# The last half blocks of a graph-attention layer: which engine normalises them, in which order GpSimd works, and where the block in front is put

## The chip, the cores and the metric

The kernel runs on one core of a Trainium2 chip. The core has five engines with a queue of instructions each: TensorE (PE in the profile; its weight loads are PEld), VectorE (DVE), ScalarE (ACT), GpSimd (POOL) and SyncE (SP), which here only issues DMAs. Each of VectorE, ScalarE, GpSimd and SyncE works its queue strictly in the order in which the program wrote it; an instruction that waits holds up all that stand behind it. Engines wait for one another by semaphores. The metric is the time of the whole program in microseconds (us), lower is better.

## The reference

One layer of masked attention on x (8 frames, 2048 nodes, 256 channels), eight heads of 32 channels, with a feed-forward part, two normalisations inside and one behind:

```python
scores = where(adj > 0, q @ k.T / sqrt(32), -1e9)        # per frame and head
t = softmax(scores) @ v
x1 = layernorm(x + t) * g1 + be1
h = relu(x1 @ w1 + b1)
x2 = layernorm(x1 + h @ w2 + b2) * g2 + be2
out = layernorm(x + x2)                                   # no scale, no shift
```

All is float32. A layernorm is (value - mean) / sqrt(variance + eps) over the 256 channels of a row.

## The kernel before, in words

The main loop runs over 1024 items: 8 frames, 4 blocks of 512 query rows, 2 groups of four heads, 16 blocks of 128 keys. Step t of the loop issues the exponential of item t+1 (ScalarE, L283), the scores of item t+2 (TensorE) with the addition of the mask (VectorE, L279), the product with the values of item t (TensorE, L310) and the sums of exponentials (GpSimd, L339, or an accumulating DMA). The very last group of heads of the last block, called ENDING, is done in two halves of 256 rows: its items 1008 to 1015 are half 0, 1016 to 1023 half 1, each item now covering two key blocks (scores L264 and L268, values L298, sums L330 and L332).

All other work stands in a list `fill` of Python generators, sorted by a due step. At the start of each step t, `advance(t)` goes through the list once. A generator that yields a number sleeps for so many steps; one that yields BANK needs a free bank of PSUM and TensorE time, and only one may have it in a step. `credit` limits that TensorE work to about one unit of 512 columns a step, unless some generator that wants a bank is past its due step: then no limit holds. A generator in the middle of a group of matmuls yields MORE, or WAIT for a step that is not there yet; it then is the `holder`, and while there is a holder at the start of a step nobody else gets a bank in that step. After step 1023 the list is worked off by `advance(t, finish=True)` for t = 1025, 1026 and so on, where any number of generators may have banks in one pass, still in the order of due steps. The order in which the passes write instructions is the order of the queues; times follow from that.

Three generators matter at the end:

- `tail` for the block in front (the third block of the last frame, whole, 512 rows; `xb` is set for it and for no other): normalise (`norm`, per=2), feed-forward, normalise, GpSimd's multiplication by g2 (L445) and addition of `xb`, which holds x + be2 (L447), normalise, store (L453). In `norm` VectorE takes statistics (L348, L349), GpSimd makes 1/sqrt and the bias (L353 to L357), ScalarE applies them (L360). `per` says how many of the four row tiles are done before it yields.
- `closing(0)` and `closing(1)`, the two halves of the last block, with due steps 1024 and 1023. Each sums its denominators on TensorE in five terms (L494) and adds them to those of the other heads (L497); turns them and the attention output, divides and adds x (L508, L526, L529); takes statistics (`half_stats`: L460, L461 on VectorE, L463, L464 on GpSimd); normalises (`half_norm`: L469, then ScalarE L471); has GpSimd make the residual for later (L535, L536) while TensorE turns the rows and ScalarE applies g1 and be1 (L541); does the two products of the feed-forward (L548 and L557, listed by the profile under the helper's line L54, with L549 between); adds the residual (L559), normalises, multiplies by g2 and adds x + be2 (L564, L565), normalises and stores (L569).

Each `yield` in `closing` ends its part of the pass. In the kernel before, half 0 gets through its denominators by step 1023, half 1 makes all its five terms in pass 1025, and half 0 is one part ahead of half 1 from there; in a pass, half 1's part is written in front of half 0's next part, because its due step is the earlier one.

Of the kernel before, what the change touches and what calls it, by code (L numbers as in the profile page):

```python
# [61 lines left out]
def fast_path(ctx, tc, cst, x, adj, out, RS):  # L62
# [339 lines left out]
    def outcome(f, qc):  # L402
        yield ROOM
        state["tails"] += 1
        xin = x[f, qc * CH:(qc + 1) * CH, :].rearrange("(p j) c -> p j c", p=P)
        y = yp.tile([P, TPC, C], F32, name="y")
        begin = items.index((f, qc, 1, LAST)) + SUM + 2
        yield from divide(f, qc, y)
        if (f, qc) == (F - 1, NCK - 2):
            xb = state["xb"]  # L410
            for j in range(0, TPC, 2):
                yield BANK
                ps = bank()
                columns(ps, ident, xb[:, j:j + 2, :].rearrange("p j c -> p (j c)"), start=True, stop=True)
                nc.vector.tensor_tensor(y[:, j:j + 2, :], ps.rearrange("p (j c) -> p j c", c=C), y[:, j:j + 2, :], ALU.add)
            start(begin + 4, tail(f, qc, y, xin, 2, xb), begin + 18)
            return
        nc.gpsimd.dma_start(y, xin, accum_op=ALU.add)
        if (f, qc) == (F - 1, NCK - 3):
            start(begin + 10, tail(f, qc, y, xin, 2), begin + 18)  # L420
        else:
            start(begin + 10, tail(f, qc, y, xin), begin + 26)
# [12 lines left out]
    def tail(f, qc, y, xin, per=1, xb=None):  # L435
        yield from norm(y, per)
        yield from feed_forward(y)
        if xb is not None:
            nc.gpsimd.tensor_tensor(xb, xb, rows(cst["be2r"]), ALU.add)
        yield 1  # L440
        z = y
        yield from norm(z, per if per == 1 else TPC)
        while xb is None and per > 1 and state["now"] % MB not in CALM:
            yield 1
        nc.gpsimd.tensor_tensor(z, z, rows(cst["g2r"]), ALU.mult)  # L445
        yield 1
        nc.gpsimd.tensor_tensor(z, z, rows(cst["be2r"]) if xb is None else xb, ALU.add)  # L447
        yield 1
        if xb is None:
            nc.gpsimd.dma_start(z, xin, accum_op=ALU.add)  # L450
            yield 7 if per == 1 else 10
        yield from norm(z, per)
        nc.sync.dma_start(out[f, qc * CH:(qc + 1) * CH, :].rearrange("(p j) c -> p j c", p=P), z)  # L453
        state["tails"] -= 1

    def half_stats(t):
        mv = small.tile([P, 2, nc.vector.BN_AGGR_DIM], F32, name="mv")
        for j in range(2):
            st = small.tile([P, nc.vector.BN_STATS_DIM], F32, name="st")
            nc.vector.bn_stats(st, t[:, j, :])  # L460
            nc.vector.bn_aggr(mv[:, j, :], st)  # L461
        rs = small.tile([P, 2], F32, name="rs")
        nc.gpsimd.tensor_scalar(rs, mv[:, :, 1], EPS, 1.0, op0=ALU.add, op1=ALU.mult)  # L463
        nc.gpsimd.tensor_tensor(rs, rs, cst["mhalf"][:, 0:2], ALU.pow)  # L464
        return mv, rs

    def half_norm(t, mv, rs):
        nb = small.tile([P, 2], F32, name="nb")
        nc.vector.scalar_tensor_tensor(nb, mv[:, :, 0], -1.0, rs, op0=ALU.mult, op1=ALU.mult)  # L469
        for j in range(2):  # L470
            nc.scalar.activation(t[:, j, :], t[:, j, :], AF.Identity, bias=nb[:, j:j + 1], scale=rs[:, j:j + 1])  # L471

    def closing(h):
        f, qc, g = ENDING
        own, part, t0 = slice(2 * h, 2 * h + 2), slice(h * HQ, (h + 1) * HQ), len(items) - MB // 2 * (2 - h)
        terms = [(5, 6), (1, 7), (0, 7), (6, 8), (7, 8)]
        dst = out[f, qc * CH + h * HQ:qc * CH + (h + 1) * HQ, :].rearrange("(p j) c -> p j c", p=P)

        def row2(v):
            return v[:, None, :].to_broadcast([P, 2, C])  # L480

        yield BANK
        ps = bank()
        for n, (block, when) in enumerate(terms):
            if n:
                yield MORE
            while state["now"] < t0 + when:
                yield WAIT
            term = PT.pop((*ENDING, block + h * MB // 2))
            state["credit"] -= 4 * CH  # L490
            for b in range(2):
                for i in range(4):
                    r = D * i
                    nc.tensor.matmul(ps[r:r + D, 0:HQ], cst["halves"][:, g, :], term[:, i, b * HQ:(b + 1) * HQ],  # L494
                                     start=(n + b == 0), stop=(n + b == len(terms)))
        dT = DT[f, qc]
        nc.vector.tensor_tensor(dT[:, part], ps[:, 0:HQ], dT[:, part], ALU.add)  # L497
        if h == 0:
            state["y"] = yp.tile([P, TPC, C], F32, name="y")
            state["ff"] = [work.tile([P, 2, CH], F32, name=n) for n in ("turned", "hT")]  # L500
        y, (yT, hT) = state["y"][:, own], state["ff"]
        xr, xb = (t[:, own] for t in state["rows"])
        def turned_sums():
            ps = bank()
            transposes(ps, [dT[:, part][:, j::2] for j in range(2)])
            den = ps[:, 0:HQ].rearrange("p (j c) -> p j c", c=P)[:, :, ::D // 2]
            rc = op.tile([P, 2, H], F32, name="rc")
            nc.vector.reciprocal(rc, den)  # L508
            return rc, den

        def count(den):
            nc.vector.tensor_tensor(RS[:, 0, own], RS[:, 0, own], den, ALU.add)
            nc.vector.tensor_tensor(RS[:, 1, own], RS[:, 1, own], den, ALU.min)

        yield 1
        if h == 0:
            yield BANK
            rc, den = turned_sums()
            count(den)
        yield BANK  # L520
        po = bank()
        transposes(po, [OT[f, qc, gg][:, part][:, j::2] for gg in range(2) for j in range(2)])
        if h:
            rc, den = turned_sums()
        for gg in range(2):
            nc.vector.tensor_tensor(y[:, :, gg * P:(gg + 1) * P].rearrange("p j (h d) -> p j h d", d=D),  # L526
                                    po[:, gg * HQ:(gg + 1) * HQ].rearrange("p (j h d) -> p j h d", h=4, d=D),
                                    rc[:, :, gg::2, None].to_broadcast([P, 2, 4, D]), ALU.mult)
        nc.vector.tensor_tensor(y, y, xr, ALU.add)  # L529
        found = half_stats(y)  # L530
        if h:
            count(den)
        yield 1
        half_norm(y, *found)
        nc.gpsimd.tensor_tensor(xr, y, row2(cst["g1r"]), ALU.mult)  # L535
        nc.gpsimd.tensor_tensor(xr, xr, row2(cst["be1b2r"]), ALU.add)  # L536
        yield BANK
        ps = bank()
        transposes(ps, [y[:, j, a * P:(a + 1) * P] for a in range(2) for j in range(2)])
        for a in range(2):  # L540
            nc.scalar.activation(yT[:, a, part], ps[:, a * HQ:(a + 1) * HQ], AF.Identity,  # L541
                                 bias=cst["be1c"][:, a:a + 1], scale=cst["g1c"][:, a:a + 1])
        yield 1
        for d in range(2):
            yield BANK
            ps = bank()
            for a in range(2):
                columns(ps[:, 0:HQ], w1s[:, a, d * P:(d + 1) * P], yT[:, a, part], start=(a == 0), stop=(a == 1))  # L548
            nc.scalar.activation(hT[:, d, part], ps[:, 0:HQ], AF.Relu, bias=cst["b1s"][:, d:d + 1], scale=1.0)  # L549
        yield 1  # L550
        yield BANK
        ps = bank()
        for j in range(2):
            if j:
                yield MORE
            for d in range(2):
                columns(ps[:, j * C:(j + 1) * C], hT[:, d, part][:, j * P:(j + 1) * P], w2s[:, d, :], start=(d == 0), stop=(d == 1))  # L557
        z = y
        nc.vector.tensor_tensor(z, ps.rearrange("p (b c) -> p b c", c=C), xr, ALU.add)  # L559
        found = half_stats(z)  # L560
        yield 1
        half_norm(z, *found)
        yield 1
        nc.vector.tensor_tensor(z, z, row2(cst["g2r"]), ALU.mult)  # L564
        nc.vector.tensor_tensor(z, z, xb, ALU.add)  # L565
        found = half_stats(z)
        yield 1
        half_norm(z, *found)
        nc.sync.dma_start(dst, z)  # L569

# [39 lines left out]
    def start(t, gen, due):  # L610
        fill.append([t, gen, 1, due])
        fill.sort(key=lambda e: e[3])
# [408 lines left out]
```

## Time and profile before

| | us |
|---|---|
| median of 3 runs | 3159.01 (3158.67 to 3160.27) |
| profiled execution, its own time | 3158.02 |
| its span, first to last instruction | 3156.0 |
| TensorE busy in the span | 3051.3 (97%), granted clock 0.994 |
| last exponential (L283) starts | 3110.35 |
| last matmul of the feed-forward (L54) ends | 3140.05 |
| last store (L569) is issued | 3151.15 |

Times inside the execution are counted from the start of the span. A row of the timeline gives start, duration, engine, line, operation, output<-input with their shapes, the number of instructions merged, and in brackets how long the engine had been idle before and what released it. What lies behind about 3110 us is the end of the program: no exponentials are left, and only the three generators above run.

### The profile page before, as it was taken

To read this page: it belongs to the slowest core of one execution; us is meant where nothing else is said; L and a number is where in the kernel's file an instruction comes from. 1 tells how busy PE (TensorE), PEld (TensorE's weight loads), DVE (VectorE), ACT (ScalarE), POOL (GpSimd) and SP (SyncE) were. 2 spreads that over 40 slices of the span, in tenths; PEclk is the share of its full clock that TensorE was granted. 3 is DMA by queue.
4 is the path that set the end of the run, shared out by engine and by line. 5 is a ranking of instruction groups with operands and counts; after the bars stand their busy time and mean duration, and the time that the engine had idled before them with its cause. 6 is when DMAs were issued, how large, how long until landed. Compare 5 with 4: busy or idle time off the path is not lost.

```text
span 3156.0 us, 68508 instructions
## 1 busy us (share of the span) xinstructions
PE 3051.3 (97%) x28988; PEld 962.6 (31%) x28988; DVE 2747.6 (87%) x3139; ACT 2427.1 (77%) x1934; POOL 2727.7 (86%) x1389
## 2 busy tenths in 40 slices
PE   8999999999999999999999999999999999999986
PEld 4222333233332233223332323323333233322223
DVE  4989888998888988888988888988888988889885
ACT  4877878777778877778777878778778778778774
POOL 1768989888889888899888899899989899899985
PEclk9999999999999999999999999999999999999998
DMA  8998878889789888789878899788888889778871
GB/s 258 223 210 185 196 170 194 193 191 198 173 174 209 197 190 178 170 195 214 192 169 187 187 207 195 166 184 204 197 176 191 190 192 202 167 173 166 173 157 42
DMA packets 165465, 586.86 MB, mean 186 GB/s; under 512 B 15360, under 2 KB 84480, under 8 KB 116512
## 3 DMA queue, kind: packets, MB, share of 16 engines
q0 software_dynamic: 63696, 430.60, 69.4%
q1 hardware_dynamic: 100640, 150.50, 14.1%
q8 instruction: 229, 3.75, 0.5%
q10 hardware_dynamic: 816, 1.31, 0.1%
q14 instruction: 84, 0.69, 0.1%
HBM read 146.15 MB, written 37.75 MB: 58 GB/s over the span
## 4 chain that ended last, share of the span: by engine, by line


## 5 line engine op out<-in xcount | busy, mean ns | idle before, releaser
L279 DVE TENSOR_TENSOR p<-s,mask 128x1024 f32<-128x1024 f32 x2016 | 2371.5, 1218 | 297.7 <-PE s L276 123.4
L283 ACT ACTIVATE p<-p 128x2048 f32<-128x2048 f32 x1024 | 1955.7, 1910 | 551.1 <-DVE p L279 449.1
L339 POOL TENSOR_TENSOR p<-p 128x2048 f32<-128x2048 f32 x409 | 1999.9, 4890 | 221.3 <-ACT p L283 200.4
L276 PE MATMUL s<-qT,kT 32*128 32x512 f32 x8064 | 1152.0, 640 | 56.5 <-DVE p L279 52.6
L310 PE MATMUL x<-p,v 128*32 128x512 f32 x8064 | 1075.8, 606 | 5.8 <-ACT p L283 4.2
L276 PEld LDWEIGHTS s<-qT,kT 32*128 32x128 f32 x8064 | 315.3, 183 | 659.5 <-DVE p L279 629.4
L336 POOL DMA_DIRECT2D p<-p x378 | 416.2, 1104 | 49.2 <-ACT p L283 41.0
L310 PEld LDWEIGHTS x<-p,v 128*32 128x32 f32 x8064 | 158.7, 108 | 771.3 <-issue 315.1
L54 PE MATMUL x<-in,wqkv 128*32 128x512 f32 x1888 | 245.7, 592 | 0.0
L383 PE MATMUL x<-p,halves 128*32 128x512 f32 x1768 | 231.1, 594 | 1.6 <-DVE kT L170 1.4
L360 ACT ACTIVATE y<-y,nb,rs 128x256 f32<-128x256 f32 x372 | 218.3, 591 | 0.5 <-POOL nb L357 0.5
L348 DVE BATCH_NORM_STATS2 st<-y 128x6 f32<-128x256 f32 x372 | 154.8, 416 | 0.0
L54 PE MATMUL x<-turned,w1s 128*32 128x512 f32 (+1 forms) x1008 | 125.2, 593 | 0.0
L54 PEld LDWEIGHTS x<-wqkv,in 128*32 128x32 f32 x3584 | 102.4, 110 | 66.5 <-issue 55.4
L54 PE MATMUL x<-w2s,hT 128*32 128x256 f32 x2048 | 122.0, 379 | 0.0
L54 PE MATMUL x<-wqkv,in 128*32 128x128 f32 x3584 | 118.2, 273 | 0.0
L54 PEld LDWEIGHTS x<-in,wqkv 128*32 128x32 f32 x1888 | 61.3, 110 | 141.3 <-issue 116.0
L354 POOL TENSOR_TENSOR rs<-rs,mhalf 128x4 f32<-128x4 f32 x93 | 96.2, 1035 | 7.8
L445 POOL TENSOR_TENSOR y<-y,g2r 128x1024 f32<-128x1024 f32 x31 | 99.3, 3205 | 2.2 <-ACT y L360 2.2
L383 PEld LDWEIGHTS x<-p,halves 128*32 128x32 f32 x1768 | 57.3, 110 | 133.9 <-issue 126.5
L447 POOL TENSOR_TENSOR y<-y,be2r 128x1024 f32<-128x1024 f32 x30 | 94.4, 3145 | 0.2
L54 PEld LDWEIGHTS x<-w2s,hT 128*32 128x32 f32 x2048 | 66.4, 110 | 69.7 <-issue 35.6
(164 smaller groups left out, 1433.6 us busy)
## 6 DMA issues: line engine op xcount, KB each, us to landing
p<-p POOLq DMA_DIRECT2D x380, 1024.0 KB, 9.1
in<-xd SPq DMA_DIRECT2D x87, 512.0 KB, 7.5
mask<-md SPq DMA_DIRECT2D x248, 128.0 KB, 5.4
y<-in_x_dram POOLq DMA_DIRECT2D x60, 512.0 KB, 10.3
out_dram<-y SPq DMA_DIRECT2D x31, 512.0 KB, 4.5
in<-in_x_dram SPq DMA_DIRECT2D x30, 512.0 KB, 6.8
xd<-in SPq DMA_DIRECT2D x28, 512.0 KB, 6.8
p<-in_adj_dram SPq DMA_DIRECT2D x8, 1024.0 KB, 14.3
```

Source lines behind the costliest of these rows:

```text
L54: nc.tensor.matmul(out[r:r + D], lhsT[:, r:r + D], rhs, start=start, stop=stop)
L276: nc.tensor.matmul(ps2[half][:, j, :], KT[f, mb // TPC, g][r:r + D, (mb % TPC) * P:(mb % TPC + 1) * P], QT[f, qc, g][r:r + D, :], start=Tr ...
L279: nc.vector.tensor_tensor(pt[:, 2 * half:2 * half + 2, :], ps, MK[f, qc, mb // 2][:, mb % 2, None, :].to_broadcast([P, 2, CH]), ALU.add)
L283: nc.scalar.activation(PT[item], PT[item], AF.Exp, scale=1.0 / math.sqrt(D))
L310: nc.tensor.matmul(O[grp][r:r + D, :], V[f, mb // TPC, g][:, mb % TPC, r:r + D], PT[item][:, h, :], start=(mb == 0), stop=(mb == LAST))
L336: nc.gpsimd.dma_start(PT[f, qc, g, chain[0]], PT.pop(item), accum_op=ALU.add)
L339: nc.gpsimd.tensor_tensor(first, first, PT.pop(item), ALU.add)
L348: nc.vector.bn_stats(st, t[:, j, :])
L354: nc.gpsimd.tensor_tensor(rs, rs, cst["mhalf"], ALU.pow)
L360: nc.scalar.activation(t[:, j, :], t[:, j, :], AF.Identity, bias=nb[:, j:j + 1], scale=rs[:, j:j + 1])
L383: nc.tensor.matmul(ps[r:r + D, :], cst["halves"][:, g, :], term[:, h, :], start=(n == 0), stop=(n == len(blocks) - 1))
L445: nc.gpsimd.tensor_tensor(z, z, rows(cst["g2r"]), ALU.mult)
```

## The change

Four things are edited, all of them at the end of the last frame.

1. The tail of the block in front is due at its begin + 14 (step 1011) instead of begin + 18 (step 1015).
2. In that tail, GpSimd's multiplication and addition are issued in the same step, and the last normalisation takes all four statistics in one step and applies all four in one (TPC is 4).
3. `half_norm` is two VectorE instructions (subtract the mean, multiply by 1/sqrt, with one number per row each) instead of one small VectorE instruction and two ScalarE activations. `closing` uses it three times per half; its middle use is dissolved: the mean and g2 are applied in one VectorE instruction per row tile without waiting for 1/sqrt, and 1/sqrt and x + be2 in a second one.
4. GpSimd's L535 and L536 are written behind the `yield 1` that follows the turning of the rows, so one pass later.

```diff
-            start(begin + 4, tail(f, qc, y, xin, 2, xb), begin + 18)
+            start(begin + 4, tail(f, qc, y, xin, 2, xb), begin + 14)
...
         nc.gpsimd.tensor_tensor(z, z, rows(cst["g2r"]), ALU.mult)
-        yield 1
+        if xb is None:
+            yield 1
         nc.gpsimd.tensor_tensor(z, z, rows(cst["be2r"]) if xb is None else xb, ALU.add)
         yield 1
         if xb is None:
             nc.gpsimd.dma_start(z, xin, accum_op=ALU.add)
             yield 7 if per == 1 else 10
-        yield from norm(z, per)
+        yield from norm(z, per if xb is None else TPC)
...
     def half_norm(t, mv, rs):
-        nb = small.tile([P, 2], F32, name="nb")
-        nc.vector.scalar_tensor_tensor(nb, mv[:, :, 0], -1.0, rs, op0=ALU.mult, op1=ALU.mult)
         for j in range(2):
-            nc.scalar.activation(t[:, j, :], t[:, j, :], AF.Identity, bias=nb[:, j:j + 1], scale=rs[:, j:j + 1])
+            nc.vector.tensor_scalar(t[:, j, :], t[:, j, :], mv[:, j, 0:1], rs[:, j:j + 1], op0=ALU.subtract, op1=ALU.mult)
...
         half_norm(y, *found)
-        nc.gpsimd.tensor_tensor(xr, y, row2(cst["g1r"]), ALU.mult)
-        nc.gpsimd.tensor_tensor(xr, xr, row2(cst["be1b2r"]), ALU.add)
         yield BANK
...
         yield 1
+        nc.gpsimd.tensor_tensor(xr, y, row2(cst["g1r"]), ALU.mult)
+        nc.gpsimd.tensor_tensor(xr, xr, row2(cst["be1b2r"]), ALU.add)
         for d in range(2):
...
-        found = half_stats(z)
-        yield 1
-        half_norm(z, *found)
-        yield 1
-        nc.vector.tensor_tensor(z, z, row2(cst["g2r"]), ALU.mult)
-        nc.vector.tensor_tensor(z, z, xb, ALU.add)
+        mv, rs = half_stats(z)
+        for j in range(2):
+            nc.vector.scalar_tensor_tensor(z[:, j, :], z[:, j, :], mv[:, j, 0:1], cst["g2r"], op0=ALU.subtract, op1=ALU.mult)
+        yield 1
+        for j in range(2):
+            nc.vector.scalar_tensor_tensor(z[:, j, :], z[:, j, :], rs[:, j:j + 1], xb[:, j, :], op0=ALU.mult, op1=ALU.add)
         found = half_stats(z)
         yield 1
         half_norm(z, *found)
```

## Prediction, made before the changed kernel was run

> **What bounds the kernel now.** The page's totals and slices come first.
>
> ```profile
> span 3156.0 us, 68508 instructions
> PE   8999999999999999999999999999999999999986
> ```
>
> TensorE is full in every slice but the ends; the change touches the last slice only, so I read that by the windows (busy time of PE, PEld, DVE, ACT, POOL, then the granted clock).
>
> ```profile
> 3110.00:3120.00 10.00, 7.67 (x120) 4.67 (x112) 2.51 (x8) 2.62 (x3) 4.73 (x2) 1.00 0.01 2
> 3120.00:3130.00 10.00, 2.21 (x7) 1.23 (x8) 6.30 (x29) 3.09 (x6) 4.65 (x7) 0.59 0.00 0
> 3130.00:3140.00 10.00, 10.00 (x133) 4.98 (x131) 1.44 (x4) 2.92 (x6) 3.81 (x6) 0.72 0.01 2
> 3140.00:3156.00 16.00, 0.24 (x8) 0.08 (x2) 7.42 (x25) 6.22 (x12) 4.36 (x8) 0.57 0.19 70
> ```
>
> Nothing is full but TensorE from 3130 to 3140, at 0.72 clock: the end is a chain across engines. The timeline, engine by engine, shows its links.
>
> ```profile
> 3113.18 4.50 PE L494 MATMUL s<-p,halves 128*32 128x256 f32 x80
> 3130.46 1.94 PE L54 MATMUL x<-turned,w1s 128*32 128x256 f32 x16
> ...
> 3117.75 0.43 DVE L497 TENSOR_TENSOR dT<-s,dT 128x256 f32<-128x256 f32 x1 [6.62 <-PE s L494]
> 3125.31 0.15 DVE L469 SCALAR_TENSOR_TENSOR nb<-mv,rs 128x2 f32<-128x2 f32 x1
> 3126.51 0.13 DVE L469 SCALAR_TENSOR_TENSOR nb<-mv,rs 128x2 f32<-128x2 f32 x1
> 3138.49 0.69 DVE L559 TENSOR_TENSOR y<-x,in 128x512 f32<-128x512 f32 x1 [11.85 <-PE x L54]
> ...
> 3128.50 1.08 ACT L471 ACTIVATE y<-y,nb,rs 128x256 f32<-128x256 f32 x2
> 3143.35 1.08 ACT L360 ACTIVATE y<-y,nb,rs 128x256 f32<-128x256 f32 x2
> ...
> 3121.69 0.71 POOL L464 TENSOR_TENSOR rs<-rs,mhalf 128x2 f32<-128x2 f32 x1
> 3129.66 1.27 POOL L535 TENSOR_TENSOR in<-y,g1r 128x512 f32<-128x512 f32 x1 [0.38 <-ACT y L471]
> 3146.19 0.54 POOL L463 TENSOR_SCALAR rs<-mv 128x2 f32<-128x2 f32 x1 [2.91 <-DVE mv L461]
> 3146.82 1.15 POOL L464 TENSOR_TENSOR rs<-rs,mhalf 128x2 f32<-128x2 f32 x1
> ...
> 3150.32 0.37 SPq L453 DMA_DIRECT2D out_dram<-y  x1
> 3151.15 0.33 SPq L569 DMA_DIRECT2D out_dram<-y  x1
> ```
>
> Half 0's 1/sqrt is ready at 3122.40 (3121.69+0.71), yet L469 starts at 3125.31: half 1's division, sum and statistics stand in front on VectorE. ScalarE then takes the norm of half 0, its turning, the norm of half 1, its turning; the feed-forward starts at 3130.46. Near the end the front block's L360 and its 512 KB store (L453) run among the halves' own.
>
> **The change, part by part.** I traced the generators by hand through `advance`.
>
> *The front block (due 1011, statistics at once).* At step 1013 it is past due, so the two last terms of the other heads' denominator go in one step and everything behind moves one step forward. Half 0's five terms come at 1018 to 1022 (1019 to 1023 before), three of half 1's go at 1023, and two are left for pass 1025. TensorE's work is the same. By its pitches (1.07 scores, 0.88 values, 0.97 a term) with the stall behind the front block's statistics (0.99, a step earlier), scores of item 1023 start at 3106.8 (3105.9 before). ScalarE's four L360 (2.06) now precede exponential 1022: values 1022 wait until 3110.2. Then values (0.88), three terms (0.87 each, from 4.50/5), values, two terms: the sums end at 3116.5, against 3117.68 before. **1.2 gained.** Queue by queue: GpSimd has L445 and L447 (2.36+2.37) behind the last L330 (about 3108.6), to 3113.5; VectorE's four statistics wait for that and end at 3115.6, in front of half 1's L497 (3116.5): 0.9 to spare. On SP the store moves from pass 1032 to 1028, ahead of both L569. The DMA L332, issued near 3102.3, lands within 8.4 (its longest), at 3110.7; its term wants it at 3112. GpSimd's L353 to L357 come before the halves' L463.
>
> *The halves' order.* Half 1 is the holder at the start of pass 1025, so half 0's turning waits for 1026. From there both run in the same pass, half 1 first. VectorE: L497 to L508 takes 1.0 (L497, two transposes); half 1's division, sum and statistics 2.86; its counts 0.14; half 0's, with counts, 0.48+1.52+1.09. Add 0.33 for the four small final-check instructions (L975 to L978) that also lie here now. That puts half 0's mean at 3124.0, its 1/sqrt 1.08 later, 3125.1.
>
> *Norms by VectorE.* No row has this form. L279 (1024 elements, two inputs) takes 1218 ns and L700 (a tensor_scalar, 1024) 691: the difference is half the streaming, so 164 fixed and 1.03 ns an element, half that in L700's fast form. For 256 elements: 296 ns if fast, 428 if not; with a per-row operand neither is shown. A pair at overlapped pitch is 0.5 or 0.76. I take the fast form, L700 being the same operation; the slow one costs 0.26 twice on the path. Half 1's norm hides behind half 0's 1/sqrt; ScalarE's two were 1.08. The scalar_tensor_tensor is taken at 0.42, L497's time for 256 elements (bounds 0.30 and 0.50).
>
> Here a rule speaks against the change. The row: L463 takes 0.54 at 3146.19 instead of 0.19, and L464 1.15 instead of 0.71, just where VectorE runs L564 and L565 with both inputs in SBUF; both end soon after a VectorE instruction does. The Trainium skill, page "SBUF — State Buffer", section "Who interferes with whom", says that GpSimd and a VectorE instruction with two SBUF inputs or in its two-port mode hold one port pair exclusively, whichever starts first. By the rows alone VectorE loses nothing; by the rule L535 (1.27), free to start when half 1 is normalised, can lodge between half 0's two norms: 1.2 more on the path. L535 starts about 0.09 after L464 and VectorE's norm 0.03 after it, so VectorE gets in first, but its second norm may not. I put 0.2 for each 1/sqrt that is slowed (twice), and keep 1.2 for the range. Moving L535 and L536 behind both halves' L463 and L464 costs nothing: four times 1.27 end by about 3131, L559 needs them at 3134.7.
>
> Half 0's norm so ends at 3125.8; its turning and copying take as long as before, and the feed-forward starts 0.88 after the norm (3129.58 to 3130.46 before): 3126.7. **2.5 more, 3.7 in all.** From there to the first L559 is 8.03 before, and the same matmuls after: 3134.7. The clock: it fell to 0.50 at 3121.9 and rose at 3135.5, so TensorE worked cold for 5.0 of these. The skill's "TensorE: Matmul & The Clock Gate", Part 1, has free-running windows of 3413 ns; 13.6 is four of them. So the rise may come anywhere in one window: 0.85 either way, kept in the range; by the row alone it is none.
>
> *From L559 to the last store.* Before 12.66 (3138.49 to 3151.15). After, all on VectorE: per half 1.83 (sum and statistics) and 0.68 (the two that apply mean and g2), then 0.68 and 1.17 (sum and statistics) per half, half 1's norm beside the last 1/sqrt, 1.28 to that with the slowing, half 0's norm 0.5: 2x2.51+2x1.85+0.08+1.28+0.53 = 10.6. **2.1 gained.** The waits for the other 1/sqrt are covered by the other half's instructions; without cover they cost 1 each.
>
> *The last transfer.* From the last issue to the end of the span is 4.85. The two L569 landed 2.4 and 3.7 after issue; the last one queues behind 512 KB issued 0.8 before it. That is gone now; the other half's 256 KB is issued about 1.1 earlier and was moved at near 390 GB/s in 0.7. I take 2.4 for it: **1.3 gained** (bounds 0 and 1.3).
>
> Sum: 1.2+2.5+2.1+1.3 = 7.1, say 7.0. The profiled execution's 3158.02 becomes 3151.0; the median of the runs lies 1.0 above that execution, so 3152.0.
>
> **The rivals.** *GpSimd gets in between.* L535 before half 0's second norm (1.2), slow tensor_scalar (0.5), late clock (0.85): 7.0 less 2 to 3, 3154 to 3155, which is within 0.2% (6.3 us; about what a measurement of this kernel can tell from no change). For it: the slowed L463; against: VectorE's durations there are undisturbed.
>
> *The front block blocks VectorE: slower.* Its statistics now stand in front of half 1's L497 and wait for GpSimd's L447; behind them is the whole closing. Beyond 0.9 every us of GpSimd's lateness is a us. At the in-loop means of L445 and L447 (3.2 and 3.1) that is 0.7 lost; it decides when GpSimd is 7.9 late, and at 15 late gives 3166. For it: L332 ahead in the queue can wait for landings (9.1 median for such DMAs); against: in this trace L332 waited 0.36 at most.
>
> *Nothing comes of it.* Swapping the halves only swaps which one waits, and the rest is lost: 3157 to 3160. Against it: two ScalarE stages and the shared 512 KB go in any case.
>
> **How the numbers follow.** The sum holds, 3149.5 to 3152.7: 0.55. GpSimd or the clock takes a part, 3152.7 to 3156.5: 0.30. Nothing: 0.05. Slower by the front block: 0.10. The range 3149.5 to 3156.5 leaves out the last two. Faster 0.55, same 0.35, slower 0.10.
>
> **What would show it.** In the changed profile: L497 of half 1 near 3116.5 with no wait for GpSimd; VectorE unbroken to half 0's norm near 3125; first w1 matmul near 3126.7; L559 near 3134.7; last L569 near 3145.3 with a landing near 2.4; L453 near 3120. Wrong if statistics (L348) are seen waiting for L447 beyond 3117, a norm is over 0.5, or the feed-forward starts after 3128.

## The result and the profile after

The changed kernel takes 3154.47 us (median of 22 runs, 3152.38 to 3156.79), the kernel before 3159.05 (22 runs): a ratio of 0.9985, 95% interval 0.9979 to 0.9991. That is 4.6 us less: inside the forecast range, short of the forecast 7.0, clear of no change, and yet within the 0.2% that the prediction calls "same".

The two profiled executions differ by some 3 us before the changed part is reached, with the same instructions up to there: the front block's second turning (TensorE, L95, step 1010) starts at 3068.37 before and at 3071.43 after. Over all kernels of this study that point lies between 3068.4 and 3071.8. So the end is counted from that turning, here and below.

| from the second turning, us | before | after | difference |
|---|---|---|---|
| half 1's sums end (TensorE) | 49.31 | 48.44 | -0.87 |
| feed-forward starts (first w1 matmul) | 62.09 | 60.45 | stretch: -0.77 |
| first addition behind it (L559, now L558) | 70.12 | 67.08 | stretch: -1.40 |
| last store issued | 82.78 | 78.00 | stretch: -1.74 |
| end of the span | 87.63 | 81.57 | stretch: -1.28 |

A stretch is the time from the line above. Together they add up to 6.06. The page's totals hardly move (line numbers behind L443 shift by one or more in the changed kernel):

```profile
span 3153.0 us, 68496 instructions
PE 3049.4 (97%) x28988; PEld 962.8 (31%) x28988; DVE 2752.0 (87%) x3145; ACT 2421.2 (77%) x1922; POOL 2728.9 (87%) x1389
```

ScalarE lost its 12 activations, VectorE is a little busier. The reading is in the timeline. First TensorE and VectorE around the sums and the feed-forward of the changed kernel:

```profile
3077.06 2.76 PE L383 MATMUL x<-p,halves 128*32 128x512 f32 x24
...
3115.35 1.93 PE L493 MATMUL x<-p,halves 128*32 128x256 f32 x32 [0.79 <-DMA p<-p]
3117.96 1.91 PE L493 MATMUL x<-p,halves 128*32 128x256 f32 x32
...
3129.80 0.45 PE L95 MATMUL s<-ident,y 128*128 128x128 f32 x1 [1.13 <-DVE y L470]
3131.05 0.90 PE L95 MATMUL s<-ident,y 128*128 128x128 f32 x3 [0.81 <-DVE y L470]
3131.88 3.04 PE L54 MATMUL x<-turned,w1s 128*32 128x256 f32 x32
...
3119.94 0.42 DVE L496 TENSOR_TENSOR dT<-x,dT 128x256 f32<-128x256 f32 x1 [0.20 <-PE x L493]
...
3127.00 0.70 DVE L470 TENSOR_SCALAR y<-y,mv,rs 128x256 f32<-128x256 f32 x2
3128.30 2.69 DVE L470 TENSOR_SCALAR y<-y,mv,rs 128x256 f32<-128x256 f32 x2 [0.59 <-POOL rs L465]
3138.51 0.69 DVE L558 TENSOR_TENSOR y<-s,in 128x512 f32<-128x512 f32 x1 [7.51 <-issue]
```

Three terms of the other heads' denominator stand in one step (x24 is three times eight), where the forecast had two. TensorE waits 0.79 for the accumulating DMA. And the two pairs of norms on VectorE, half 1's and then half 0's, the same instruction on the same shape, take 0.70 and 2.69. GpSimd beside them:

```profile
3127.18 0.26 POOL L464 TENSOR_SCALAR rs<-mv 128x2 f32<-128x2 f32 x1 [2.17 <-DVE mv L462]
3127.52 0.75 POOL L465 TENSOR_TENSOR rs<-rs,mhalf 128x2 f32<-128x2 f32 x1
3128.24 1.27 POOL L541 TENSOR_TENSOR in<-y,g1r 128x512 f32<-128x512 f32 x1
3129.58 1.26 POOL L542 TENSOR_TENSOR in<-in,be1b2r 128x512 f32<-128x512 f32 x1
3131.07 1.27 POOL L541 TENSOR_TENSOR in<-y,g1r 128x512 f32<-128x512 f32 x1 [0.23 <-DVE y L470]
```

Half 1's L541 starts at 3128.24, directly behind the 1/sqrt that half 0's norms wait for. VectorE's pair starts at 3128.30. The rows of its first norm go to TensorE at 3129.80, after L541's end (3129.51), and the pair ends at 3130.99, just after L542's end (3130.84). Half 0's turning waits for these norms, and the first product of the feed-forward stands behind that turning.

SyncE's timeline of the changed kernel has the stores; the last line, for the two L568, is the time from issue to landing:

```profile
3123.86 0.34 SPq L454 DMA_DIRECT2D out_dram<-y  x1
3148.11 1.66 SPq L568 DMA_DIRECT2D out_dram<-y  x2
DMA to landing us min/median/max: 2.0/2.2/2.3
```

Then windows of 2 us, two of the kernel before and four of the changed one (the granted clock is the third number from the end):

```profile
3120.00:3122.00 2.00, 0.00 (x0) 0.00 (x0) 1.86 (x8) 0.00 (x0) 0.50 (x2) 0.96 0.00 0
3134.00:3136.00 2.00, 2.00 (x32) 0.93 (x28) 0.00 (x0) 0.67 (x2) 0.20 (x1) 0.62 0.03 8
...
3122.00:3124.00 2.00, 0.00 (x0) 0.00 (x0) 1.86 (x9) 1.80 (x4) 0.00 (x0) 0.98 0.00 0
3124.00:3126.00 2.00, 0.00 (x0) 0.00 (x0) 2.00 (x12) 0.00 (x0) 0.90 (x2) 0.50 0.64 262
3132.00:3134.00 2.00, 2.00 (x20) 0.86 (x24) 0.00 (x0) 1.13 (x3) 1.61 (x2) 0.50 0.00 0
3134.00:3136.00 2.00, 2.00 (x40) 1.15 (x36) 0.00 (x0) 0.97 (x3) 0.00 (x0) 0.96 0.04 8
```

The front block's 512 KB are issued 25.6 us before the last store, which now lands in 2.0 to 2.3. The clock fell at 3123.9 and was back by 3134.2, 2.3 us after the feed-forward began; in the kernel before it was back 5.0 after.

### The profile page after: what moved, and what is told of

Same layout as the page of the kernel before. It is cut to its first block, busy times and chain, and to the rows that moved or that the text cites. A ratio compares the mean times of both kernels' runs of the same rounds, so it can differ in the third digit from the quotient of the medians.

```text
span 3153.0 us, 68496 instructions
## 1 busy us (share of the span) xinstructions
PE 3049.4 (97%) x28988; PEld 962.8 (31%) x28988; DVE 2752.0 (87%) x3145; ACT 2421.2 (77%) x1922; POOL 2728.9 (87%) x1389
## 5 line engine op out<-in xcount | busy, mean ns | idle before, releaser
L279 DVE TENSOR_TENSOR p<-s,mask 128x1024 f32<-128x1024 f32 x2016 | 2371.5, 1218 | 296.8 <-PE s L276 123.4
L582 POOL TENSOR_TENSOR y<-y,be1b2r 128x1024 f32<-128x1024 f32 x31 | 86.7, 2797 | 0.1
```

Source lines behind the costliest of these rows:

```text
L279: nc.vector.tensor_tensor(pt[:, 2 * half:2 * half + 2, :], ps, MK[f, qc, mb // 2][:, mb % 2, None, :].to_broadcast([P, 2, CH]), ALU.add)
```

## The experiments

All are the changed kernel with one edit, but where it is said. Times inside are from one profiled execution each, counted from the second turning. The ratio is to the kernel before in runs on the same chip (its medians there: 3158.33 for e1, e2, e4 and e5; 3159.14 for e3, e6, e7 and e9; 3159.42 for e11).

| kernel | sums end | feed-forward | first L558 | last store | end | ratio (95%) |
|---|---|---|---|---|---|---|
| changed | 48.44 | 60.45 | 67.08 | 78.00 | 81.57 | 0.9985 (0.9979 to 0.9991) |
| e1_queue | 48.09 | 58.19 | 64.24 | 75.16 | 78.79 | 0.9978 (0.9969 to 0.9987) |
| e2_due16 | 48.05 | 60.06 | 68.17 | 79.09 | 82.67 | 0.9984 (0.9975 to 0.9994) |
| e4_scalar_first | 48.36 | 60.63 | 67.74 | 78.67 | 82.22 | 0.9990 (0.9980 to 0.9999) |
| e5_early_pool | 47.77 | 60.14 | 66.68 | 77.60 | 81.15 | 0.9984 (0.9975 to 0.9994) |
| e3_due18 | 49.31 | 61.05 | 67.83 | 78.75 | 82.36 | 0.9982 (0.9973 to 0.9992) |
| e6_front_only | 48.65 | 60.92 | 67.70 | 80.28 | 84.24 | 0.9994 (0.9985 to 1.0003) |
| e7_closing_only | 49.31 | 61.56 | 68.04 | 79.41 | 84.13 | 0.9995 (0.9985 to 1.0004) |
| e9_warm | 48.15 | 57.85 | 65.05 | 75.98 | 79.61 | 0.9977 (0.9968 to 0.9986) |
| e11_warm50 | 47.95 | 57.82 | 63.34 | 74.26 | 77.80 | 0.9970 (0.9959 to 0.9982) |

The intervals overlap for most pairs of these kernels. What tells them apart is the trace, and there the stretch from the feed-forward to L558 depends on the clock of that one execution (5.5 to 8.1; see "The clock").

### GpSimd's scale and shift behind both halves' norms

In this cut and the one of e5_early_pool, `<L541, L542>` stands for the two GpSimd instructions of these lines.

```diff
         yield 1
-        <L541, L542>
+        if h == 0:
+            <L541, L542>
         for d in range(2):
...
         yield 1
+        if h:
+            <L541, L542>
         yield BANK
```

> The changed kernel with one edit: half 1's L541 and L542 (GpSimd's scale and shift) are written one pass later, so that in GpSimd's queue they stand behind half 0's, which cannot start before half 0 is normalised. In the changed kernel's trace half 0's two norms on VectorE took 2.69 us where half 1's took 0.70. Theory A (GpSimd's L541 and L542 held the port pair): half 0's pair takes 0.7 to 0.8, the feed-forward starts 1.9 us sooner after the statistics, and the time falls by 1.9 to about 3152.5, ratio to the kernel before 0.9979. Theory B (the norm is slow for another reason, such as its operand read): still 2.7, no change in time, 3154.5.

Time 3151.07. The timeline of e1_queue, VectorE and GpSimd (its L542 is the L541 of the changed kernel), and all eight norms:

```profile
3125.08 0.70 DVE L470 TENSOR_SCALAR y<-y,mv,rs 128x256 f32<-128x256 f32 x2
3126.38 0.74 DVE L470 TENSOR_SCALAR y<-y,mv,rs 128x256 f32<-128x256 f32 x2 [0.59 <-POOL rs L465]
...
3125.59 0.75 POOL L465 TENSOR_TENSOR rs<-rs,mhalf 128x2 f32<-128x2 f32 x1
3127.19 1.27 POOL L542 TENSOR_TENSOR in<-y,g1r 128x512 f32<-128x512 f32 x1 [0.85 <-DVE y L470]
...
L470 DVE TENSOR_SCALAR y<-y,mv,rs x8: 380/408/413, 3125.1 to 3144.5; 128x256 f32<-128x256 f32 x8
```

GpSimd now idles 0.85 until half 0 is normalised, and the second pair takes 0.74: 1.95 less. The feed-forward starts 2.26 sooner (0.35 of it the sums), the end comes 2.78 sooner, nearly all the rest being a clock that rose earlier. Theory A holds: nothing about the norms was changed, only what GpSimd ran beside them. The traces fit the exclusive port pair of the Trainium skill's "SBUF — State Buffer", "Who interferes with whom", where whoever issues first holds it for the whole instruction: in the changed kernel L541 started 0.06 before the norm. It cost two waits of about the length of a GpSimd instruction, not one.

### Which form the norm runs in

At the end of e1_queue, behind the last store, on a dead tile:

```diff
+            for n in (256, 512, 1024):
+                nc.vector.tensor_scalar(t[:, 0:n], t[:, 0:n], mv[:, 0, 0:1], rs[:, 0:1], op0=ALU.subtract, op1=ALU.mult)
+            for n in (256, 512, 1024):
+                nc.vector.tensor_scalar(t[:, 0:n], t[:, 0:n], 0.5, 0.25, op0=ALU.subtract, op1=ALU.mult)
```

> e1_queue with six tensor_scalar instructions on VectorE behind the last store, on a tile that is no longer used: 256, 512 and 1024 elements with one number per row each for the mean and the scale (as in half_norm), then the same three with constants. The output is not touched; the time is at most some 2 us longer. Theory A (half_norm runs in the fast form[...], with some 0.1 us for its row operands): steps of 0.13 from 256 to 512 and 0.27 from 512 to 1024 in both, the first three some 0.1 longer. Theory B (row operands put it into the slow form): 0.27 and 0.53 with row operands, half of that with constants. GpSimd is idle there.

Durations of the three with row operands (one number per row, for the mean and for the scale), then of the three with constants (ns; shortest, middle and longest are 256, 512 and 1024 elements):

```profile
L577 DVE TENSOR_SCALAR in<-in,mv,rs x3: 407/547/811, 3146.3 to 3147.3; 128x256 f32<-128x256 f32 x1, 128x512 f32<-128x512 f32 x1, 128x1024 f32<-128x1024 f32 x1
L579 DVE TENSOR_SCALAR in<-in x3: 294/427/694, 3148.1 to 3148.9; 128x256 f32<-128x256 f32 x1, 128x512 f32<-128x512 f32 x1, 128x1024 f32<-128x1024 f32 x1
```

Steps of 140 and 264 with row operands, 133 and 267 with constants: both are the fast form, about 0.52 ns an element against the 1.03 worked out for L279, and two row operands add 113 to 120 per instruction. Theory A. With constants the 256 elements take 294, within 2 of the prediction's working; with row operands 407, in between its two values. (The one time, 3153.76, holds the extra work and a late clock.)

### The front block one step sooner instead of two

```diff
-            start(begin + 4, tail(f, qc, y, xin, 2, xb), begin + 14)
+            start(begin + 4, tail(f, qc, y, xin, 2, xb), begin + 16)
```

> The changed kernel with begin + 16 in place of begin + 14. The tail then moves one step forward instead of two: the schedule that the prediction traced. Theory A (GpSimd's queue): L330 of item 1018 stands in front of the tail's L353 again and does not wait for it, L332 is issued some 4 us sooner, half 1's second term does not wait for its DMA (0.79 in the changed kernel), the sums end 0.3 to 0.8 sooner and so does the program: 3153.9. Theory B (TensorE's work alone sets the end of the sums): within 0.2 of the changed kernel, 3154.5. Half 0's norms still take about 2.7 in both.

Time 3153.80. In its trace the sums end at 48.05, 0.39 sooner, and TensorE has no wait for the DMA:

```profile
3098.01 4.57 POOL L330 TENSOR_TENSOR p<-p 128x2048 f32<-128x2048 f32 x1 [6.26 <-ACT p L283]
3102.66 0.19 POOL L353 TENSOR_SCALAR rs<-mv 128x4 f32<-128x4 f32 x1
3104.84 0.92 POOL L332 DMA_DIRECT2D p<-p  x1 [0.30 <-issue]
...
3113.22 2.77 PE L493 MATMUL x<-p,halves 128*32 128x256 f32 x48
```

L332 is issued at 34.3 from the turning, against 35.7 in the changed kernel, where L353 to L357 stood in front of L330. So A is right in direction, but L332 moved by 1.4 and not by 4: here L353 to L357 still stand between L330 and L332. The end (82.67) is later all the same, because this execution's clock rose late: 8.11 from the first product to L558, 6.63 in the changed kernel. The times do not tell the two apart.

### The first norm back on ScalarE

```diff
-        half_norm(y, *found)
+        <the bias on VectorE and two activations on ScalarE, as in the kernel before>
```

> The changed kernel with the first of the three norms (of y) back on ScalarE, as in the kernel before; all else as changed. [...]nothing of GpSimd's is in its way, but its queue takes half 1's norm, half 1's turning, and only then half 0's norm. Theory A (port pair, queue order): half 0's norm ends about 0.4 later than in the changed kernel, 3154.9, which says that the move to VectorE gained nothing here because the port pair took it back. Theory B (VectorE's norm is what gained): 2 us slower, 3156.5.

Time 3155.09. The feed-forward starts at 60.63, 0.18 later than in the changed kernel: theory A. ScalarE's two pairs take 1.09 and 1.08, the second beside a GpSimd instruction of 1.26. In this place moving the norm to VectorE gained next to nothing, because ScalarE's own queue (norm, turning, norm, turning) and the port pair cost about the same. With the port pair free, as in e1_queue, the feed-forward starts 2.44 sooner than here (60.63 to 58.19), 0.27 of it by sooner sums.

### GpSimd's two in their old place

```diff
         half_norm(y, *found)
+        <L541, L542>
         yield BANK
...
         yield 1
-        <L541, L542>
```

> The changed kernel with L541 and L542 written in front of the turning again (edit 4 undone). GpSimd's queue has the same order and nothing stands between, so the prediction's step says no change: 3154.5, within 0.3 in the trace, half 0's norms 2.7. Rival: moving them behind did keep them out of the way of half 1's norms, and undoing it costs up to 1.2.

Time 3152.79, end 81.15; half 0's pair again takes 2.69, beside half 1's scale (L534 here):

```profile
3126.75 1.26 POOL L534 TENSOR_TENSOR in<-y,g1r 128x512 f32<-128x512 f32 x1
...
3126.82 2.69 DVE L470 TENSOR_SCALAR y<-y,mv,rs 128x256 f32<-128x256 f32 x2 [0.59 <-POOL rs L465]
```

No change, as forecast. Edit 4 moves the instructions in the program but passes nothing in GpSimd's queue, and half 1's L541 has all its inputs as soon as half 1 is normalised. It stands behind both halves' 1/sqrt, as the prediction meant it, with the edit or without; behind half 0's norm it does not.

### Undoing and isolating the parts

```diff
e3_due18:        begin + 14  ->  begin + 18
e6_front_only:   the kernel before with edits 1 and 2
e7_closing_only: the changed kernel without edits 1 and 2
```

> The changed kernel with begin + 18 again (edit 1 undone, statistics at once kept). Half 0's sums end by step 1023 and it leads half 1 by a pass again. Counted from the second turning of the front block (step 1010), the changed kernel's span ends at 81.6 us, the kernel before at 87.6. Theory A (queues): sums end at 49.3 as before; half 0's norm waits behind half 1's statistics on VectorE, GpSimd's L541 of half 0 now stands in front of half 1's norm, which takes 2 to 2.7; the feed-forward starts near 61.5, the end is near 82.7, the time 3155.5. Theory B (which half is ahead decides): the feed-forward starts near 62, as before, the end is near 84, 3157. If the step forward is worth nothing: 81.6, 3154.3.

> The kernel before with edits 1 and 2 alone (front block sooner, statistics at once); norms and GpSimd's L535 and L536 as before. From the second turning: sums end at 48.4, the norms of the two halves follow one another on ScalarE, the feed-forward starts at 60.6, no L360 stands between the halves' norms, the last store is alone (3.6 from issue to end instead of 4.85). End near 83.7, time 3156.2. If the front edits only matter with the norms on VectorE, 87, 3158.

> The changed kernel with edits 1 and 2 undone: only the norms on VectorE and GpSimd's two moved. From the second turning: sums end at 49.3, half 0 leads, half 1's norm meets GpSimd's L541; feed-forward near 61.5, first addition behind it near 69, last store 11 later, the front block's 512 KB store still close to the last one, so 4.6 to the end: near 84.6, time 3156.5. If the parts add up with the front-only kernel, the two gains sum to the changed kernel's 6.0; if they overlap, to more.

Times 3154.79, 3157.18 and 3157.29. Each end lies within 0.6 of what was expected (82.36, 84.24, 84.13). In e3_due18 half 0 leads, and now half 1's norms meet half 0's L541:

```profile
3128.96 1.26 POOL L541 TENSOR_TENSOR in<-y,g1r 128x512 f32<-128x512 f32 x1
...
3129.02 2.69 DVE L470 TENSOR_SCALAR y<-y,mv,rs 128x256 f32<-128x256 f32 x2 [0.87 <-POOL rs L465]
```

The second pair takes 2.69 again, only the half is another. So the order of the halves does not matter to the port pair. Edit 1 is worth 0.87 at the sums and 0.79 at the end of these traces; the times do not show it (0.9982 without it, 0.9985 with it).

The two groups of edits alone gain 3.4 (front) and 3.5 (closing) at the end of the traces, both together 6.1. But each of these traces had a shorter cold stretch than the kernel before, and that counts once in each. By the medians they gain 2.0 and 1.9 alone, 4.6 together; neither group alone is clear of no change, so that they add up is not shown.

### The clock

```diff
         if h:
             rc, den = turned_sums()
+        else:
+            idle = bank()
+            for _ in range(30):      # e11_warm50: 50
+                nc.tensor.transpose(idle[:, 0:P], ident, ident)
```

Both are added to e1_queue.

> The kernel with half 1's L541 and L542 behind half 0's (e1_queue), and 30 transposes of the identity on TensorE into a bank that nobody reads, in the gap between the turning of the attention output and the turning of the normalised rows (5.8 us idle in e1_queue, about 5 of it filled). Theory (clock): the granted clock stays at 1.00, the two turnings take 0.65 instead of 1.2, the feed-forward starts 0.6 sooner and its first part loses the slow 0.8, the end from the second turning falls from 78.8 to 77.4, the time from 3151.1 to about 3149.7. Rival (the clock costs nothing on this path, VectorE and GpSimd set it): no change, 78.8; if the extra work stands in front of the turning, later.

> As e9_warm with 50 idle transposes in place of 30. There the 30 ran at 0.11 us each and left 2.6 us of TensorE idle; the clock fell at 58.3 us behind the front block's second turning, just as the feed-forward began, and rose one window later. 50 take 5.7 and end within 0.4 of the turning of half 1's rows. Theory (clock): granted clock 1.00 throughout, first feed-forward product near 57.7, first addition behind it (L558 of the changed kernel) near 63.0, end near 77.6, against 78.8 in e1_queue; time about 3150. Rival (the clock falls whatever the filling): 79 to 79.6, 3151 to 3152. If the 50 run past 55.8, the turning and all behind it are late by so much.

e9_warm missed: 3152.11, end 79.61. The 30 transposes took 3.44 instead of 5, and the clock fell just after the feed-forward began. Windows of e9_warm:

```profile
3126.00:3128.00 2.00, 1.45 (x15) 0.74 (x17) 0.73 (x2) 1.47 (x3) 1.15 (x2) 0.95 0.00 0
3128.00:3130.00 2.00, 2.00 (x24) 1.08 (x20) 0.00 (x0) 1.05 (x3) 1.92 (x3) 0.50 0.03 8
3130.00:3132.00 2.00, 2.00 (x32) 1.08 (x28) 0.00 (x0) 0.48 (x2) 1.92 (x2) 0.70 0.00 0
```

TensorE was full from 3128 to 3132 and slow for most of it. e11_warm50 closes the gap, in its timeline of TensorE:

```profile
3119.03 5.62 PE L527 MATMUL s<-ident 128*128 128x128 f32 x50
3125.09 0.78 PE L95 MATMUL s<-ident,y 128*128 128x128 f32 x4 [0.43 <-DVE y L470]
3127.12 1.07 PE L54 MATMUL x<-turned,w1s 128*32 128x256 f32 x16
```

and in its window over the feed-forward's first products the clock stays at 1.00:

```profile
3126.00:3130.00 4.00, 3.58 (x60) 2.21 (x64) 0.59 (x2) 2.91 (x7) 3.25 (x3) 1.00 0.01 4
```

Time 3149.62, ratio 0.9970: the end at 77.80, the feed-forward to L558 in 5.52, against 8.03 in the kernel before and 6.05 to 8.11 in all other kernels without filling. That the clock costs time on this path is shown, and how much: in each of the twelve profiled executions this stretch, less half of the time that the clock stood at 0.50 in it, is 5.5 to 5.7. Before, that is 8.03 less half of 5.05; after, 6.63 less half of 2.30. e12_sizes has the same instructions as e1_queue up to its last store and took 7.14 for the stretch, e1_queue 6.05: executions of one path differ by that much.

This version is 9.8 us under the kernel before on its chip, the best ratio of all; against e1_queue the traces differ by 1.0 at the end, while the intervals of the times overlap.

## Why the prediction was right, and where it was not

The range (3149.5 to 3156.5) held the time, and the rival of that price, GpSimd in between, 3154 to 3155, is what took place. The likeliest case ("faster", 7.0) was too good by 2.4. Of the prediction's own signs of being wrong two came: a norm of over 0.5 (up to 1.42), and a feed-forward after 3128 (3128.8 in its frame). By its steps, in its own frame (add 3068.37):

- *The front block.* The step "two last terms of the other heads' denominator go in one step and everything behind moves one step forward" failed: three terms went at step 1012, and everything moved two steps. `advance` asks `more()` a second time for the holder inside its loop over the list, after the tail, overdue, has come to its BANK; I had traced only the first place. With begin + 16 (e2_due16) the traced schedule came, with sums at 48.05, where the prediction had 48.1 (3116.5). As built they ended at 48.44: the tail's L353 to L357 stood in front of L330 on GpSimd, L332 was 1.8 later than reckoned (35.7 against 33.9), and TensorE waited 0.79. Gained 0.87, not 1.2. VectorE made up the missing 0.3: half 0's mean stood at 55.66, against 55.6 forecast.
- *VectorE's spare time in front of L497.* 0.9 was forecast. The statistics ended at 48.30 from the turning, L496 started at 48.51: 0.2 left, none in e1_queue, e5_early_pool and e11_warm50 (L496 0.15 to 0.47 behind the sums). The slower rival was nearer than its 7.9 us of margin said, but a few tenths are all that it took.
- *Norms by VectorE.* This is the term that was mis-sized, and it holds the whole shortfall up to the feed-forward. Put at 0.5 for the pair and 0.2 for each 1/sqrt, with 1.2 for L535 kept for the range. Measured: 0.70 for a pair without L541 and L542 beside it, 2.69 with them. GpSimd's instruction was ready to start as its 1/sqrt ended, 0.06 before VectorE's, and went first; its second followed before VectorE's second. "VectorE gets in first", reckoned from gaps in the trace before, was wrong. The rule of the port pair weighed there held, and at 1.95 its price was above the 1.2 allowed. The feed-forward began at 60.45, not at 58.3; e1_queue, with the port free, had 58.19. L700, from which the fast form was taken, has constants and another type; by e12_sizes the form is right and the row operands were left out.
- *Feed-forward to L559.* Forecast unchanged at 8.03, 0.85 either way for the clock; it came at 6.63, and over eight further kernels without filling at 6.05 to 8.11. The clock fell at 3121.9 and rose at 3135.5 before, 3123.9 and 3134.2 after, four and three times the 3.4 of the one cold stretch of e9_warm (3127.8 to 3131.2). So 1.4 of the 6.06 in the two traces is where these windows happened to lie; 6.06 - 1.40 = 4.66 is left, close to the 4.58 of the medians. That the medians average over it is argued from this, not shown.
- *From L559 to the last store.* 10.6 forecast, 10.92 measured: the pairs took 0.70 to 0.87 at overlapped pitch instead of 0.5 and 0.68. Unbroken on VectorE but for the last 1/sqrt (0.59 idle), as said.
- *The last transfer.* 1.3 forecast, 1.28 measured; landing 2.0 to 2.3 against 2.4.
- *L535 and L536 moved.* "Costs nothing" was right (e5_early_pool): the edit changed nothing in the queue, and so it did not keep them out of the way either.

So 7.1 less 2.1 (the feed-forward at 60.45 instead of 58.33, all of it at half 0's norms) and less 0.3 (10.92 instead of 10.6) leaves 4.7, the stretches of the trace without the clock's 1.4. The agreement to a tenth with the medians is partly luck; the interval of the gain is 2.8 to 6.6 us. So is the agreement with the rival's 3154 to 3155: it reckoned with one GpSimd instruction in front of half 0's second norm, a slow tensor_scalar and a late clock; what came was two of them, one in front of each norm, a fast tensor_scalar and, in the trace, an earlier clock.

## What to carry to other kernels

An instruction that is written later is not later: if it passes nothing in its queue and its inputs are there, it starts as before; to keep it back, put it behind something that waits. When an elementwise step moves from ScalarE to VectorE, look at what GpSimd has ready at that moment: here the two norms lost about a whole GpSimd instruction each, more than the step itself. At a tail of small dependent steps, count from a common point inside the trace, since the microseconds in front of it differ from run to run by as much as the change is worth. And a gap in TensorE can have its price only later: here 5.8 us of idle time (e1_queue) slowed the products behind it, and filling helped only when it left 0.43 (e11_warm50), not when it left 2.6 (e9_warm).

## What was not expected of the hardware

- Two waiting VectorE instructions and two GpSimd instructions came to their ends in turn: L541, a norm, L542, the other norm. Only VectorE lost by it: a norm took up to 1420 ns, against 380 to 413 undisturbed in e1_queue, while L541 and L542 took 1.27 and 1.26, as they do elsewhere.

```profile
L470 DVE TENSOR_SCALAR y<-y,mv,rs x8: 381/408/1420, 3127.0 to 3149.0; 128x256 f32<-128x256 f32 x8
```

- Row operands cost a tensor_scalar 113 to 120 ns more than constants (407, 547, 811 against 294, 427, 694).
- The clock fell in e9_warm at 3127.8 although TensorE had been idle for 2.6 at most and had worked again since 3125.4; with 0.55 of idle time at most (e11_warm50) it stayed at 1.00 through the feed-forward.
